# A four-layer image network on one core: layer 1's input and dt products in scan order on two partition halves, and PSUM pairs of layers 2 and 3 read by one engine after the other

## The chip, the core and the metric

The kernel runs on one core of a Trainium2 chip. The metric is the device time of one execution, in microseconds (us), median of the runs. The engines named below are PE (matrix products), DVE (VectorE), ACT (ScalarE), POOL (GpSimd) and SP, whose queue issues nearly all transfers. Each engine takes its instructions strictly in the order in which the program lists them.

## The reference, cut to what matters

The input is 16 images of 96 channels and 56 x 56 positions (L = 3136). Four layers follow each other. Layer 0 is a masked inverted-residual convolution. Layer 1 is a selective scan (below). Layers 2 and 3 each take the Fourier transform of the tokens, a diagonal complex product with ReLU, the inverse transform, and then a small quantized MLP. Everything is float32 but that MLP.

Layer 1, for what the change touches (Din = 192, R = 6, N = 1, four scan directions):

```python
xs = jnp.stack([xf, xt, xf[..., ::-1], xt[..., ::-1]], axis=1)   # xt: the image turned (w before h)
dbl = jnp.einsum('bkdl,kcd->bkcl', xs, x_proj_w)
dts, Bs, Cs = jnp.split(dbl, [R, R + N], axis=2)
dt = jax.nn.softplus(jnp.einsum('bkrl,kdr->bkdl', dts, dt_projs_w) + dt_projs_b[None, :, :, None])
a = jnp.exp(dt[:, :, :, None, :] * A[None, :, :, :, None])
bb = dt[:, :, :, None, :] * Bs[:, :, None, :, :] * xs[:, :, :, None, :]
_, h = jax.lax.associative_scan(comb, (a, bb), axis=-1)
y = jnp.einsum('bkdnl,bknl->bkdl', h, Cs) + Ds.reshape(K, Din)[None, :, :, None] * xs
```

Layers 2 and 3, the part that the change touches (X is the Fourier transform of 192 columns):

```python
xr = jax.nn.relu(X.real * rd - X.imag * idg + rb)
xi = jax.nn.relu(X.imag * rd + X.real * idg + ib)
```

## The kernel before, in words

Three functions run one after the other: `layer0`, `layer1` and `layers23` (layers 2 and 3 together). Inside each, several tasks are written as Python generators. A task yields an `Op` (engine, a cost, a delay, buffers that it takes and gives back), and then issues the instructions of that step. The function `in_order` is a list planner: it always advances the task whose next step can start first by the costs and by the buffers that are free in its books. The order in which the steps come out is the order of the instructions on every engine; there is no other scheduler. So a changed cost, buffer count or step order can move every instruction after it. Which semaphore an instruction waits for is worked out afterwards from the data and the buffers, and not from the costs. Two engines that read the same PSUM tile are also kept apart.

PSUM is used as four pairs of banks (tag `ps`), each of 2 x 512 float32 values per partition.

**Layer 1** has five tasks over the images: `fronts` (norm, in-projection, depthwise convolution, inputs of the scan), `makes` (dt and a), `drives`, `scans` and `backs` (out-projection and MLP).

- The convolution (L783) runs on quarters of the array: 64 rows to 64 columns, four different quarters in turn, into two banks (`p_c`). Its result, u, lies in two tiles: u0 with 128 channels, and u1 with the last 64 channels twice, in its lower half as the image lies and in its upper half turned.
- `inputs` (L811 to L829) makes `proj`, one tile [128, 3136]. Its 128 rows are four groups of 32, one per scan direction, of which 8 are used (6 for dt, then B and C), and one row that `k_one` makes 1 for the dt bias. Seven blocks of 448 columns go through PE, two products each (`xp0`, `xp1`, L819 and L820). ACT writes the lower 64 rows as they come (L822) and the upper 64 rows turned (L827), so that each direction's columns lie in its own order.
- Four transfers (L836) copy the B and C rows to a DRAM tile `bc`; later transfers (`rb`, `rc`, L882 and L886) read them back, spread over 128 partitions.
- `made_of` takes twelve units per image (six channel tiles, two halves of the sequence), each in two pieces of 784 columns. For each piece PE makes two products of 392 columns with all 128 rows of `proj` (L860, `p_d`), ACT takes softplus of the pair (L862, `dt`), and later exp of it (L871, `a`). Softplus, exp and gelu (L1042) need different tables, and a change of table is an instruction of its own.
- DVE multiplies by u (L915), by B (L919), runs the scan (L939, L941), multiplies by C (L946) and adds up (L953, L958). There is one `proj` buffer, five `dt` and two each of `a`, `rb` and `rc`.

**Layers 2 and 3** run three images at a time, as three tasks. `first_half` transposes, multiplies (`p_a` L1262), DVE takes ReLU times the norm (`h`, L1265), PE makes the first transform (`p_1`, L1271), ACT copies it (`y`, L1274) and SP writes it out. `middle` reads it back (`z`) and, in `unit`, makes the second transform in a PSUM pair (L1293) and the complex product: ACT c (L1300), then two child tasks, `imaginary` (DVE L1311 and L1313, ACT L1316, DVE L1318) and `real` (ACT L1322 and L1325, DVE L1327 and L1330), which the planner interleaves freely. Six of these nine read the pair: L1300, L1322 and L1325 on ACT, L1311, L1313 and L1327 on DVE. `back` follows (`p_v` L1341 and L1342, `vv` L1345, `p_u` L1352, `uu` L1355, written out), then `added` reads it back (`z4`) for the last transform (L1388). The tiles `h`, `y`, `vv`, `uu` (two each) and `z4` (three) are of nearly one size and have each their own buffers.

Of the kernel before, what the change touches and what calls it, by code (L numbers as in the profile page):

```python
# [43 lines left out]
ALU = mybir.AluOpType  # L44
# [44 lines left out]
def packed(x):  # L89
# [28 lines left out]
    xp = np.zeros((P, 2 * P), f)  # L118
    wdt = np.zeros((P, 6, P), f)
    o["k_one"] = np.zeros((P, 1), f)  # L120
    for to, k in enumerate((0, 2, 1, 3)):
        xp[32 * to : 32 * to + R + 2, :DIN] = w("x_proj_w")[k]
        o["k_one"][32 * to + R + 2] = 1.0
        for i, halves in enumerate(TILES):
            at = 0
            for of, n in halves:
                if of == k:
                    d = slice(0, P) if n == P else slice(P, DIN)
                    wdt[32 * to : 32 * to + R, i, at : at + n] = w("dt_projs_w")[k, d].T
                    wdt[32 * to + R + 2, i, at : at + n] = w("dt_projs_b")[k, d]  # L130
                at += n
    o["l1_xp0"], o["l1_xp1"], o["l1_dt"] = xp[:, :P].T, xp[:, P:].T, wdt
# [425 lines left out]
def layer1(ctx, tc, src, given, dst):  # L558
# [7 lines left out]
        "ps": 4, "x": 1, "half": 1, "xc": 2, "big": 7, "proj": 1, "dt": 5, "a": 2, "rb": 2, "rc": 2, "xn": 1,  # L566
# [10 lines left out]
    n1, n2, no, xp0, xp1, wdt, kone, ds, fc1b, fc2, fc2b = ph.loads(  # L577
        "l1_n1", "l1_n2", "l1_no", "l1_xp0", "l1_xp1", "l1_dt", "k_one", "l1_d", "l1_fc1b", "l1_fc2", "l1_fc2b"
# [96 lines left out]
    def front(b, it):  # L675
# [135 lines left out]
        it["proj"] = proj = buf([P, L], "proj")  # L811

        def inputs(g):
            banks = 2 if g < 3 else 1
            yield pe(2 * banks, 0.75)
            p = pair("p_x")
            for b in range(banks):
                cols = slice(896 * g + T * b, 896 * g + T * b + T)
                nc.tensor.matmul(p[:, b, :T], xp0, us[0][:, cols], start=True, stop=False)  # L819
                nc.tensor.matmul(p[:, b, :T], xp1, us[1][:, cols], start=False, stop=True)  # L820
            yield act(T * banks, over=0.16)
            nc.scalar.activation(  # L822
                proj[:64, 896 * g : 896 * g + T * banks].rearrange("p (b n) -> p b n", n=T), p[:64, :banks, :T],
                AF.Identity, bias=kone[:64],
            )
            yield act(T * banks, 1.95e-3, give=("ps",))
            nc.scalar.activation(  # L827
                turned(proj[64:])[:, 16 * g : 16 * g + 8 * banks].rearrange("p (b h) w -> p b h w", h=8),
                p[64:, :banks, :T].rearrange("p b (h w) -> p b h w", w=S), AF.Identity, bias=kone[64:],  # L829
            )  # L830

        yield [inputs(g) for g in range(4)]
        it["bc"] = bc = dram.tile([4, 2, L], F32, tag="bc", name="bc")
        yield Op("SP", 1.4, 4.0, post=it["ready"])
        for g in range(4):
            nc.sync.dma_start(bc[g], proj[32 * g + 6 : 32 * g + 8])  # L836
# [6 lines left out]
    def made_of(it):  # L843
# [4 lines left out]
        def steps():  # L848

            for unit in units:  # L850
                i, h = unit
                order = (0, 1) if i < 3 else (1, 0)
                for s in order:
                    yield Op("none", 0.0, 0.0, take=("dt",))
                    made[unit][s] = dt = buf([P, SUB], "dt")
                    yield pe(2, 0.66)
                    p = pair("p_d")
                    for b in range(2):
                        cols = slice(HALF * h + SUB * s + TC * b, HALF * h + SUB * s + TC * b + TC)
                        nc.tensor.matmul(p[:, b, :TC], wdt[:, i], proj[:, cols], start=True, stop=True)  # L860
# [244 lines left out]
def layers23(ctx, tc, src, given, dst):  # L1105
# [9 lines left out]
        "ps": 4, "xn": 2, "xt": 2, "h": 2, "y": 2, "z": 3, "na": 2, "nc": 2, "gg": 6, "vv": 2, "uu": 2,  # L1115
        "z4": 3, "xq": 2, "y16": 2, "h8": 2, "o16": 2, 
    }
    buf = lambda shape, tag, dtype=F32: work.tile(shape, dtype, tag=tag, name=tag, bufs=buffers[tag])

    ident = ph.c([P, P], "ident")  # L1120
# [128 lines left out]
    def first_group(t, w, d1, m0, k, r):  # L1249
# [8 lines left out]
        def quad(at, give):  # L1258
            yield pe(4, 0.325, ("ps", "h"), give)
# [4 lines left out]
            h = buf([Q, 4, HW], "h")  # L1264
# [3 lines left out]
            yield pe(4, 0.325, ("ps",), ("h",))  # L1268
# [3 lines left out]
            yield act(4 * HW, take=("y",), give=("ps",))  # L1272
            y = buf([P, 4, HW], "y")
# [5 lines left out]
            yield Op("none", 0.0, 0.0, give=("y",))  # L1279
# [3 lines left out]
    def middle(w, d1, d2):  # L1283
# [4 lines left out]
        def unit(k, flat, gs, give):  # L1288
# [7 lines left out]
            xr, xi = p[:, :, :S], p[:, :, S:Q]  # L1296
            yield act(448, over=0.25, take=("nc",))
# [3 lines left out]

            open_ = [2]

            def read():
                open_[0] -= 1
                if open_[0] == 0:
                    yield Op("none", 0.0, 0.0, give=("ps",))

            def imaginary():
                yield dve(448, over=0.13)  # L1310
                nc.vector.scalar_tensor_tensor(gi, xi, rd[:, col], c, ALU.mult, ALU.add)  # L1311
                yield dve(448, over=0.13)
                nc.vector.scalar_tensor_tensor(c, xi, rd[:, col], c, ALU.mult, ALU.subtract)  # L1313
                yield from read()
# [5 lines left out]
            def real():  # L1320
                yield act(448, over=0.16)
                nc.scalar.activation(gr, xi, AF.Abs, scale=idg[:, col])  # L1322
                yield act(448, over=0.25, take=("na",))
                a = buf([P, 8, S], "na")
                nc.scalar.activation(a, xr, AF.Relu, bias=rb2[:, col], scale=rd2[:, col])  # L1325
                yield dve(448, over=0.13)
                nc.vector.scalar_tensor_tensor(gr, xr, rd[:, col], gr, ALU.mult, ALU.add)  # L1327
                yield from read()
# [187 lines left out]
```

## Time and profile before

| | us |
|---|---|
| median of 10 runs | 7990.64 |
| lowest and highest | 7981.21, 7999.29 |
| the profiled execution: its time | 7990.78 |
| its span in the profile | 7989.0 |

The same execution by stage (the limits are rounded; busy us of each engine):

| stage, us | PE | DVE | ACT | granted PE clock |
|---|---|---|---|---|
| 0 to 1790, layer 0 | 1686.03 | 1595.39 | 825.81 | 0.98 |
| 1790 to 5290, layer 1 | 3040.23 | 2819.68 | 2475.66 | 0.92 |
| 5290 to 7989, layers 2 and 3 | 2343.35 | 1920.38 | 1637.03 | 0.94 |

A line of the profile's groups reads: line of the kernel, engine, operation, output<-inputs, shape, count | busy us, mean ns of one | idle us of the engine before them and what ended that. A line of waits reads: waiting engine, tile and line <- what it waited for: total us, times, longest. A timeline line begins with the start and the length in us. A float32 product shows as two records of MATMUL, so two products are "x4". In a shape such as 64*64 the first number counts rows of the array, the second columns.

### The profile page before, as it was taken

Reading aid. Unit: us, or ns where it says so; the run is one execution under the profiler, and the core shown is the slowest. Engines: PE = TensorE matmul, PEld = TensorE weight load, DVE = VectorE, ACT = ScalarE, POOL = GpSimd, SP = SyncE. Lnnn points to the kernel's source line nnn. Section 1 sums busy time; section 2 is a strip of 40 time slices with the busy share of each in tenths; the row PEclk is TensorE's granted clock in tenths of the full one; section 3 lists DMA queues with packets and bytes.
Section 4 is the critical chain, followed back from the end, with each engine's and each line's share of the span. In section 5 each row is a group of like instructions: output and inputs, shape, how many; then the busy total and the mean of one; then the engine's idle time right before and its main releaser. Section 6 shows DMA issues by size and latency. Waiting matters only on the chain. (4 is left out here: it accounts for less than half of the span.)

```text
span 7989.0 us, 124748 instructions
## 1 busy us (share of the span) xinstructions
PE 7069.6 (88%) x50410; PEld 4930.4 (62%) x50410; DVE 6335.5 (79%) x8036; ACT 4938.5 (62%) x6249; POOL 999.7 (13%) x798
## 2 busy tenths in 40 slices
PE   7999999987889898888889998768889989998896
PEld 3444444444556566666666665558788878887785
DVE  8999999955888888888888888636777777777765
ACT  4444444436777777777777777425666666666664
POOL 0000000000111111111111111111111111111111
PEclk9999999988899999999999999879899999999997
DMA  1000000013434344434434443235455455555552
GB/s 33 25 24 25 25 25 25 11 30 98 119 113 123 116 122 118 119 117 122 116 116 118 117 116 111 74 80 121 97 121 126 113 119 133 116 118 118 125 116 61
DMA packets 502387, 743.89 MB, mean 93 GB/s; under 512 B 208225, under 2 KB 337553, under 8 KB 498370
## 3 DMA queue, kind: packets, MB, share of 16 engines
q1 hardware_dynamic: 500770, 732.59, 35.4%
q8 instruction: 398, 6.52, 0.3%
q0 software_dynamic: 1040, 3.32, 0.1%
q14 instruction: 179, 1.47, 0.1%
HBM read 543.75 MB, written 191.99 MB: 92 GB/s over the span
## 5 line engine op out<-in xcount | busy, mean ns | idle before, releaser
L509 DVE SCALAR_TENSOR_TENSOR h<-pad,l_dw,h 128x1568 f32<-128x1568 f32 x704 | 1273.2, 1845 | 7.5
L481 PE MATMUL p_c<-pad,taps 64*64 64x392 f32 x8064 | 691.1, 492 | 2.7 <-ACT pad L462 1.9
L1235 POOL TENSOR_TENSOR r<-v,nhalf 112x16 f32<-112x16 f32 (+1 forms) x128 | 398.7, 3119 | 2261.3 <-DVE v L1233 1695.6
L860 PE MATMUL p_d<-proj,l_dt 128*128 128x392 f32 x1536 | 627.9, 536 | 46.1 <-ACT proj L827 13.1
L915 DVE TENSOR_TENSOR dt<-dt,big 128x784 f32<-128x784 f32 x384 | 456.0, 1187 | 219.3 <-ACT a L871 219.2
L481 PEld LDWEIGHTS p_c<-pad,taps 64*64 64x64 f32 x8064 | 300.2, 133 | 383.7 <-issue 354.1
L862 ACT ACTIVATE dt<-p_d 128x784 f32<-128x784 f32 x384 | 314.6, 823 | 240.1 <-PE p_d L860 233.4
L1293 PE MATMUL p<-k_f,z 112*128 112x112 f32 x3072 | 391.4, 289 | 72.7 <-DMA z<-d 57.9
L497 ACT ACTIVATE h<-p_c,shift 128x392 f32<-128x392 f32 x336 | 226.2, 673 | 366.5 <-PE p_c L481 363.0
L860 PEld LDWEIGHTS p_d<-proj,l_dt 128*128 128x128 f32 x1536 | 292.4, 207 | 254.8 <-issue 84.5
L456 PE MATMUL p<-x,l_w 96*128 96x448 f32 (+3 forms) x1280 | 426.5, 513 | 19.1 <-DVE y L546 12.0
L1293 PEld LDWEIGHTS p<-k_f,z 112*128 112x128 f32 x3072 | 384.2, 205 | 80.8 <-issue 50.1
L1048 PE MATMUL p_g<-l_fc,hid 128*112 128x96 f32 x2688 | 380.4, 276 | 43.0 <-ACT hid L1042 34.1
L1341 PE MATMUL p_v<-w,gg 128*112 128x97 f32 x2048 | 374.7, 265 | 26.6 <-DVE gg L1330 14.3
L783 PE MATMUL p_c<-x,taps 64*64 64x392 f32 x4608 | 393.8, 491 | 0.0
L1048 PEld LDWEIGHTS p_g<-l_fc,hid 128*112 128x112 f32 x2688 | 330.4, 188 | 100.9 <-ACT hid L1042 83.5
L804 ACT COPY big<-p_c 64x392 f32<-64x392 f32 (+1 forms) x448 | 267.9, 598 | 175.8 <-PE p_c L783 171.4
L946 DVE TENSOR_TENSOR dt<-a,rc 128x784 f32<-128x784 f32 x384 | 373.3, 972 | 3.8
L1039 PE MATMUL p_f<-zt,w_fc 96*128 96x448 f32 x672 | 329.0, 633 | 51.3 <-ACT zt L1033 51.3
L919 DVE TENSOR_TENSOR dt<-dt,rb 128x784 f32<-128x784 f32 x384 | 372.4, 970 | 2.2
L1342 PE MATMUL p_v<-w2both,gg 128*112 128x97 f32 x2048 | 372.9, 264 | 0.0
L531 PE MATMUL p<-h,l_w 128*96 128x392 f32 x1024 | 363.4, 497 | 10.6 <-ACT h L512 10.6
(283 smaller groups left out, 17173.3 us busy)
## 6 DMA issues: line engine op xcount, KB each, us to landing
rb<-bc SPq DMA_DIRECT2D x256, 392.0 KB
rc<-bc SPq DMA_DIRECT2D x256, 392.0 KB
d<-y SPq DMA_DIRECT2D x448, 192.0 KB
z<-d SPq DMA_DIRECT2D x128, 672.0 KB
rb<-bc SPq DMA_DIRECT2D x256, 196.0 KB
rc<-bc SPq DMA_DIRECT2D x256, 196.0 KB
d<-uu SPq DMA_DIRECT2D x256, 169.8 KB
z<-d SPq DMA_DIRECT2D x192, 194.0 KB
```

The lines of the kernel that those rows point to most:

```text
L456: nc.tensor.matmul(p[n * i : n * i + n, t, :size], w1[:, P * j : P * j + n], images[b]["x"][:, cols], start=True, stop=True,)
L481: nc.tensor.matmul(p[to : to + 64, t, :TC], taps[64 * s : 64 * s + 64, j, i], pad[64 * s : 64 * s + 64, r0 : r0 + 7, i % 3 : i % 3 + S], s ...
L509: nc.vector.scalar_tensor_tensor(out, view, dw[:, j, i : i + 1], out, ALU.mult, ALU.add)
L783: nc.tensor.matmul(p[to : to + 64, b, :TC], taps[64 * s : 64 * s + 64, j, k], pad[64 * s : 64 * s + 64, r0 : r0 + 7, k % 3 : k % 3 + S], s ...
L860: nc.tensor.matmul(p[:, b, :TC], wdt[:, i], proj[:, cols], start=True, stop=True)
L915: nc.vector.tensor_tensor(as_own(dt), as_own(dt), own(u), ALU.mult)
L946: nc.vector.tensor_tensor(dt, a, made["rc", s], ALU.mult)
L1048: nc.tensor.matmul(p[:Q, q, :C], hid[:, j, own], fc2[:, j], start=j == 0, stop=False)
L1235: nc.gpsimd.tensor_tensor(r, v, nhalf[:, :n], ALU.pow)
L1293: nc.tensor.matmul(p[:, q, :Q], flat[:, P * (3 * q + k) : P * (3 * q + k) + P], f2, start=True, stop=True)
L1341: nc.tensor.matmul(out, gs[2 * h][:, at + k], w["w2"][:, 2 * h], start=True, stop=False)
L1342: nc.tensor.matmul(out, gs[1][:, at + k], w["w2both"][:, h], start=False, stop=True)
```

## The change

**Layer 1.** `proj` becomes [128, 1568]: the sequence is cut in eight pieces of 392, even ones on partitions 0 to 63 and odd ones on 64 to 127. Each half holds four directions of 16 rows (8 used, and the bias row). `inputs` becomes two groups; for each of two banks and three weights it makes two products of 392 columns into the two column halves of the array. The second weight reads u0 turned, so the turned directions come out in their own order, and ACT writes each pair with one activation. The B and C rows go out in eight transfers instead of four. A dt piece is two products over 64 rows each (rows 0 to 63 for the first bank, 64 to 127 for the second), with the weights on both halves; the planner's cost of the pair goes from 2 x 0.66 to 1 x 0.7. `proj` gets two buffers.

**Layers 2 and 3.** In `unit`, ACT's three reads of the pair come first, then DVE's three, in one sequence, and only the rest is left to two children. `na` and `nc` get three buffers instead of two. The tiles `h`, `y`, `vv`, `uu` and `z4` are replaced by nine tiles `v` that all five uses take in turn, the one that was given back first being used first.

```diff
 # packed(): weights of layer 1
+    xp = np.zeros((3, P, 64), f)
     for to, k in enumerate((0, 2, 1, 3)):
-        xp[32 * to : 32 * to + R + 2, :DIN] = w("x_proj_w")[k]
-        o["k_one"][32 * to + R + 2] = 1.0
+        own = slice(16 * to, 16 * to + R + 2)
+        xp[to // 2, :, own] = w("x_proj_w")[k, :, :P].T
+        xp[2, 64 * (to // 2) : 64 * (to // 2) + 64, own] = w("x_proj_w")[k, :, P:].T
+        o["k_one"][[16 * to + R + 2, 64 + 16 * to + R + 2]] = 1.0
...
 # layer1
-        "ps": 4, "x": 1, "half": 1, "xc": 2, "big": 7, "proj": 1, "dt": 5, "a": 2, "rb": 2, "rc": 2, "xn": 1,
+        "ps": 4, "x": 1, "half": 1, "xc": 2, "big": 7, "proj": 2, "dt": 5, "a": 2, "rb": 2, "rc": 2, "xn": 1,
...
         def inputs(g):
+            yield pe(6, 0.66)
             p = pair("p_x")
+            for b in range(2):
+                for k in range(3):
+                    for to in range(2):
+                        c = 4 * g + 2 * b + to
+                        u = us[k // 2]
+                        from_ = turned(u)[:, 7 * c : 7 * c + 7] if k == 1 else u[:, TC * c : TC * c + TC]
+                        out = p[64 * to : 64 * to + 64, b, :TC]
+                        if k == 1:
+                            out = out.rearrange("p (w h) -> p w h", h=S)
+                        nc.tensor.matmul(out, xp[:, k], from_, start=k == 0, stop=k == 2)
+            yield act(SUB, over=0.16, give=("ps",))
             nc.scalar.activation(
+                proj[:, SUB * g : SUB * g + SUB].rearrange("p (b n) -> p b n", n=TC), p[:, :, :TC],
+                AF.Identity, bias=kone,
             )
...
         for g in range(4):
-            nc.sync.dma_start(bc[g], proj[32 * g + 6 : 32 * g + 8])
+            for to in range(2):
+                row = 64 * to + 16 * g + 6
+                nc.sync.dma_start(
+                    bc[g].rearrange("k (c n) -> k c n", n=TC)[:, to::2],
+                    proj[row : row + 2].rearrange("k (c n) -> k c n", n=TC),
+                )
...
-                    yield pe(2, 0.66)
+                    yield pe(1, 0.7)
                     p = pair("p_d")
+                    at = (HALF * h + SUB * s) // 2
                     for b in range(2):
-                        cols = slice(HALF * h + SUB * s + TC * b, HALF * h + SUB * s + TC * b + TC)
-                        nc.tensor.matmul(p[:, b, :TC], wdt[:, i], proj[:, cols], start=True, stop=True)
+                        on = slice(64 * b, 64 * b + 64)
+                        nc.tensor.matmul(p[:, b, :TC], wdt[on, i], proj[on, at : at + TC], start=True, stop=True)
...
 # layers23
-        "ps": 4, "xn": 2, "xt": 2, "h": 2, "y": 2, "z": 3, "na": 2, "nc": 2, "gg": 6, "vv": 2, "uu": 2,
-        "z4": 3, "xq": 2, "y16": 2, "h8": 2, "o16": 2, 
+        "ps": 4, "xn": 2, "xt": 2, "v": 9, "z": 3, "na": 3, "nc": 3, "gg": 6, "xq": 2, "y16": 2, "h8": 2, "o16": 2,
...
+    vs = [ph.c([P, 8 * C1], f"v{i}") for i in range(buffers["v"])]
...
-            h = buf([Q, 4, HW], "h")
+            h = quad_of(v)[:Q]
...
 # unit, in its new order
             yield act(448, over=0.25, take=("nc",))
             nc.scalar.activation(c, xr, AF.Identity, bias=ib[:, col], scale=idg[:, col])
+            yield act(448, over=0.16)
+            nc.scalar.activation(gr, xi, AF.Abs, scale=idg[:, col])
+            yield act(448, over=0.25, take=("na",))
+            a = buf([P, 8, S], "na")
+            nc.scalar.activation(a, xr, AF.Relu, bias=rb2[:, col], scale=rd2[:, col])
+            yield dve(448, over=0.13)
+            nc.vector.scalar_tensor_tensor(gi, xi, rd[:, col], c, ALU.mult, ALU.add)
+            yield dve(448, over=0.13)
+            nc.vector.scalar_tensor_tensor(c, xi, rd[:, col], c, ALU.mult, ALU.subtract)
+            yield dve(448, over=0.13, give=("ps",))
+            nc.vector.scalar_tensor_tensor(gr, xr, rd[:, col], gr, ALU.mult, ALU.add)
...
-            v = buf([Q, 8, C1], "vv")
+            v = oct_of(own)[:Q]
...
-            yield Op("SP", 0.7, 5.5, take=("z4",))
-            z = buf([P, 8, C1], "z4")
+            yield Op("SP", 0.7, 5.5, take=("v",))
+            v = vs.pop(0)
+            z = oct_of(v)
```

## The prediction

> **What bounds it now.** I read the page's slices first.
>
> ```profile
> PE   7999999987889898888889998768889989998896
> DVE  8999999955888888888888888636777777777765
> PEclk9999999988899999999999999879899999999997
> ```
>
> No stage has an engine that is simply full: layer 1 (slices 9 to 26) has PE at 8 to 9 and DVE at 8, layers 2 and 3 (the rest) have PE at 9 and DVE at 7. So I cut one repeating stretch out of each. In layer 1 five successive stretches of 208.2 us hold the same counts, one image each; in layers 2 and 3 two images repeat every 317.5 us. From the windows view (span, then PE, PEld, DVE, ACT, POOL busy, clock, DMA):
>
> ```profile
> 3429.20:3637.40 208.20, 188.19 (x1300) 126.65 (x1299) 176.61 (x212) 155.49 (x192) 33.74 (x31) 0.94 0.40 117
> 6125.40:6442.90 317.50, 286.40 (x2334) 256.58 (x2333) 238.22 (x386) 204.02 (x276) 49.97 (x16) 0.98 0.53 121
> ```
>
> In both PE is busiest, at 90%, and loses the rest to waits. DVE follows at 85% in layer 1. What DVE and ACT wait for in layer 1 (the first line over four images, the second over one; total, times, longest):
>
> ```profile
> DVE dt L915 <- ACT a L871: 68.0, 32, 8.2
> ACT dt L862 <- PE p_d L860: 16.9, 10, 4.0
> ```
>
> DVE stands 17.0 us per image for the exp of dt, out of 31.6 idle; ACT stands 16.9 us for the dt product that PE has not come to. PE is the late one. The groups of one image that the change touches, in the same view (count, then busy us and mean ns):
>
> ```profile
> L860 PE MATMUL p_d<-proj,l_dt 128*128 128x392 f32 x98 | 40.5, 538 | 2.2 <-DVE v L999 1.0 <-ACT half L759 0.9 <-ACT dt L862 0.4
> L862 ACT ACT_TABLE_LOAD x13 | 16.7, 1283 | 0.2
> L827 ACT ACTIVATE proj<-p_x,k_one 64x896 f32<-64x896 f32 (+1 forms) x4 | 6.7, 1720 | 0.1
> L822 ACT ACTIVATE proj<-p_x,k_one 64x896 f32<-64x896 f32 (+1 forms) x4 | 3.5, 906 | 0.1
> ```
>
> **Layer 1, dt products.** A pair of products is four records. From the timeline (start, length):
>
> ```profile
> 3009.30 1.48 PE L860 MATMUL p_d<-proj,l_dt 128*128 128x392 f32 x4
> 3010.62 0.74 PE L1048 MATMUL p_g<-l_fc,hid 128*112 128x96 f32 x6
> ...
> 4824.18 6.16 PE L783 MATMUL p_c<-half,taps 64*64 64x392 f32 x72
> 4830.27 1.58 PE L860 MATMUL p_d<-proj,l_dt 128*128 128x392 f32 x4
> 4831.78 6.16 PE L783 MATMUL p_c<-x,taps 64*64 64x392 f32 x72
> 4837.76 6.11 PE L783 MATMUL p_c<-half,taps 64*64 64x392 f32 x72
> 4843.80 1.58 PE L860 MATMUL p_d<-proj,l_dt 128*128 128x392 f32 x4
> ```
>
> A pair costs 1.32 us start to next start. Do two 64-row halves run side by side? The convolution answers: 72 records of the same 392 columns on quarters of the array take 5.98 us (4831.78 to 4837.76), not 72 x 0.33 = 23.8, so four quarters overlap, among them both row halves into the same columns and different banks, as the new pair does. I take 0.66 us per pair: 24 pairs x 0.66 = 15.8 us less PE per image.
>
> Changing the way the array is split costs something: p_d to p_c takes 1.51 us instead of 1.32, and p_c to p_d 6.09 (4824.18 to 4830.27) where p_c to p_c takes 5.98: 0.19 and 0.11, on average 0.15. By the order of the changed program there are 319 runs of dt products; 261 lie between full-array products (two new changes each), 30 have one such side, so 552 new changes. At 0.15 that is 83 us over 16 images, 5.2 per image. Net 10.6 us per image; bounds 9.2 (all at 0.19) and 15.8 (none).
>
> The Trainium skill, "TensorEngine Tiling (Array Packing)", Key Properties, says that changing the tiling mode drains TensorE. That speaks against this change; the rows above show the price at 0.11 to 0.19 us. The page has no figure for it.
>
> **Layer 1, inputs.** Out go 14 products of 448 columns, 0.75 us each by the timeline (10.5). In come 24 of 392 columns, two column halves side by side: 12 x 0.66 = 7.9, and 0.6 for four changes. Eight of them (four slots) read u turned, each element 224 bytes on, which no PE row shows. The nearest rows are ACT's: 1.72 turned (L827) against 0.91 plain (L822), 1.9 times. So 0 to 0.6 x 4 = 2.4; I take 2.4, since DVE's turned rows pay too. Net 10.9 - 10.5 = 0.4 more PE work. ACT loses 6.7 + 3.5 = 10.2 us and gets 2 activations of 784 columns, 0.82 each by L862's activation: 8.6 less. The order has 34 more table loads, 34 x 1.283 = 43.6 us, 2.7 per image: ACT goes from 155.5 to about 149.6 and stays under the others. SP issues 8 bc transfers instead of 4, about 0.25 us each, ahead of the rb and rc reads queued behind them: 1 us once per image, hidden since the second proj tile lets them go out before the old image's last exp; without that cover it is 1 us per image, 16 in all.
>
> The Trainium skill, "ScalarE: Activation LUTs", What ACT_TABLE_LOAD costs, adds a drain of about 1.38 us to each load. Here an exp starts 0.01 us after its load (3028.11 + 1.28, then 3029.40) and the load 0.02 us after the activation before it, so no drain shows; by the page the 34 loads would be 90 us, also on an engine with room.
>
> **Layer 1, sum.** PE falls from 188.2 to 188.2 - 10.6 + 0.4 = 178.0 us, level with DVE's 176.6. Two ways to price that. Directly: eight stops of DVE per image, each served 0.36 (0.66 less two changes) to 0.66 us earlier: 2.9 to 5.3. By load: now the busiest engine fills 188.2/208.2 = 0.904 of the period; at the same share 178.0 gives 196.9, 11.3 us less. The cap is the whole 17.0. I take 9, near the load figure, because PE's queue gets ahead and not only the one product shorter. dt products run from 1847 to 5073 in the trace, 15.5 periods: 15.5 x 9 = 140. The first image's inputs lie bare (p_x starts at 1831.3, bc goes out at 1845.9): about 5 us less. What is late next: DVE itself.
>
> **Layers 2 and 3.** Now both engines take turns on one PSUM pair; waits of two periods:
>
> ```profile
> ACT gg L1322 <- DVE gg L1311: 16.0, 24, 1.1
> ACT na L1325 <- DVE gg L1311: 8.1, 12, 0.8
> DVE nc L1313 <- ACT na L1325: 19.3, 26, 1.3
> ACT y L1274 <- DMA d<-y: 6.2, 5, 2.1
> ...
> PE p_v L1341 <- DVE gg L1330: 3.7, 2, 1.8
> PE p_v L1341 <- DVE gg L1327: 1.6, 4, 0.4
> PE p_x L1457 <- DVE gg L1327: 1.1, 2, 0.5
> ```
>
> L1322 needs nothing of L1311, nor L1313 of L1325, except the pair. Three reads by ACT and then three by DVE leave one handover. The first three lines are 43.4/2 = 21.7 us per period, but on engines with 79 (DVE) and 113 us (ACT) to spare. What reaches PE are the last three: 6.4/2 = 3.2 us per period. From 5303 to 7946 there are 8.3 periods: 27 us. Moving DVE's first read behind two more ACT reads (637 and 730 ns in the groups view) delays gi, which PE only needs at p_v; the third na and nc tiles cover that, and without them it is up to 1.4 us per unit on ACT and DVE, not on PE.
>
> The shared v tiles: by the order, 125 of 224 products h (DVE) now also wait for a transfer, and 51 of 128 evacuations v (ACT); none did. Behind h on DVE stands every other image's work, and p on PE waits for h. Nine tiles in turn should be long released; I take 0. The nearest row is y's own wait: 6.2/5 = 1.24 us each.
>
> **Sum.** The profiled execution took 7990.78 us, 0.14 over the median, span 7989.0. 7990.8 - 140 - 5 - 27 = 7819.
>
> **Rivals.** (B) DVE packs tightly: PE ahead everywhere, all 17.0 us gone, 15.5 x 17.0 = 264, and a third of PE's 31.1 idle in layers 2 and 3, 10 x 8.3 = 83: 7990.8 - 264 - 5 - 83 = 7639. For it: nothing else makes DVE wait over 4 us per image. Against: layer 1 never fills an engine past 0.904.
>
> (C) Only the direct term comes. The clock could do it: at 2100 to 2300 us PE is busy 0.86 and the clock is 0.90, against 0.94 at 0.904, so a PE with more gaps is a slower PE; 4% of 178.0 is 7 us, most of the 10.2 gained. Then 15.5 x 2.9 = 45, 5 and nothing in layers 2 and 3: 7941.
>
> (D) Slower: h on DVE waits for transfers of the tile's last user. 28 x 125/224 = 15.6 such waits per period; at 2.1 us, y's longest, and with no slack left before PE, 32.8 x 8.3 = 272 against 145: 8118. At 1.24 us it is 161, 8007. It decides from about 1.1 us per wait. Against: PE stands for h only 3.5 us in two periods.
>
> (E) The halves do not run side by side. Then PE gets 5.2 (changes) and 8.3 (24 x 0.66 + 0.6 + 2.4 - 10.5) more: 201.7/0.904 = 223.1, 14.9 x 15.5 = 231 later: 8195 with the 27. The quarters of the convolution speak against it.
>
> **Chances.** Forecast 0.55 (7819, its own range 7740 to 7900), B 0.14, C 0.17, D 0.10, E 0.04. The range 7635 to 8005 takes in C and B, and leaves out E and most of D. A run of this kernel tells 0.2%, 16 us, from no change. Faster: forecast, B and nearly all of C, 0.83; within 0.2%: 0.04, the edges of C and D; slower 0.13.
>
> **What would show it.** Right: p_d on 64 rows with 0.66 to 0.85 us start to next; PE near 178 and the layer-1 period near 199; DVE's wait for exp near 8 us per image; no waits between ACT's and DVE's first reads of a pair. Wrong: p_d still 1.3; the clock well below 0.94 in layer 1; DVE h or ACT v ended by DMA for more than 10 us per period; the period of layers 2 and 3 above 317.5.

## The result, and the profile after

The changed kernel takes 8161.93 us in the median of 8 runs (8127.41 to 8177.35), the kernel before 7989.69: a ratio of 1.0209, with an interval of 1.0198 to 1.0219. It is slower by 172 us, where 171 us less had been forecast. One of the four executions of a later kernel (order and shared tiles, 7921.04) ran at a granted clock of 0.818 instead of 0.942 and took 8523.04 us; its ratio leaves it out, and without it the median is 7919.22.

The profiled execution took 8177.35 us, with a span of 8175.6, 186.6 us over that of before. Cut at the first product `p_a` of layers 2 and 3, this divides as follows: layers 0 and 1 end at 5528.0 instead of 5314.3 (214 later), and layers 2 and 3 take 2647.6 instead of 2674.7 (27 less). So the forecast for layers 2 and 3 came out to the microsecond, by luck, as the experiments show, and the loss lies in layer 1.

The slices of the page after:

```profile
PE   7999999987888888888888888658899998999996
DVE  8999999937877777777877777945777777677765
PEclk9999999987899888888888888768999999999997
```

In layer 1 (slices 9 to 27 here) DVE fell from 8 to 7, and the clock from 9 to 8: everything there is less dense, PE as well as DVE. The windows view of 2500 to 5000 us, which is layer 1 in both kernels (span, then PE, PEld, DVE, ACT, POOL busy, clock, DMA), after:

```profile
2500.00:5000.00 2500.00, 2156.05 (x14662) 1382.44 (x14664) 1934.36 (x2323) 1673.13 (x2096) 473.74 (x331) 0.86 0.37 107
```

and before:

```profile
2500.00:5000.00 2500.00, 2247.20 (x15425) 1507.94 (x15424) 2131.00 (x2535) 1870.30 (x2304) 407.48 (x350) 0.94 0.40 117
```

DVE issues 2323 instructions instead of 2535 in the same time, 8% fewer, and PE, DVE and ACT all wait more. What the waits end on, in the same window (total, times, longest), after:

```profile
DVE dt L924 <- ACT a L880: 259.4, 65, 15.9
DVE z L1060 <- PE p_g L1058: 111.3, 41, 8.8
DVE v L1007 <- ACT o L999: 92.4, 48, 5.1
...
ACT o L999 <- PE p_o L994: 161.4, 41, 8.5
ACT dt L871 <- PE p_d L869: 62.3, 65, 2.7
ACT L871 <- DVE big L967: 48.5, 10, 5.2
ACT L880 <- DVE a L950: 43.3, 22, 3.5
...
PE p_o L994 <- ACT ysq L984: 84.2, 22, 5.1
```

and the same pairs before (DVE, ACT, PE; L915 is now L924, L862 is L871, L871 is L880):

```profile
DVE dt L915 <- ACT a L871: 185.8, 87, 11.3
DVE z L1051 <- PE p_g L1049: 46.6, 30, 5.8
DVE v L998 <- ACT o L990: 36.0, 24, 5.0
...
ACT dt L862 <- PE p_d L860: 195.8, 113, 5.1
ACT o L990 <- PE p_o L985: 56.8, 34, 3.8
...
PE p_o L985 <- ACT ysq L975: 25.6, 20, 1.8
```

The wait that the change aims at has shrunk as meant: ACT stands 62.3 us for `p_d` instead of 195.8. But DVE's wait for exp of dt has grown, with fewer and longer stops (259.4 us in 2500/226.3 = 11 periods, 23.5 us each, where about 8 had been forecast; before, 185.8 in 12 periods, 15.5 each), and a circle of waits through the out-projection and the MLP has grown with it: DVE for `p_g` and `o`, ACT for `p_o`, PE for `ysq`. The two lines "ACT L871" and "ACT L880" have no tile: they are table loads. The groups view of the whole execution shows how ACT stands before them, after (last column: idle time before, and what ended it):

```profile
L871 ACT ACT_TABLE_LOAD x244 | 313.1, 1283 | 55.9 <-DVE big L967 51.5 <-DVE big L962 0.4
L880 ACT ACT_TABLE_LOAD x192 | 246.3, 1283 | 100.1 <-DVE a L950 67.5 <-DVE dt L955 23.1 <-DVE a L948 7.1
```

and before:

```profile
L862 ACT ACT_TABLE_LOAD x216 | 277.1, 1283 | 4.1
L871 ACT ACT_TABLE_LOAD x192 | 246.3, 1283 | 41.5 <-DVE a L941 26.2 <-DVE dt L946 7.2 <-DVE a L939 4.9
```

The idle time of ACT before these loads goes from 45.6 to 156.0 us. ACT reaches the softplus and exp of coming units while DVE still works on the tiles that they would overwrite, and everything that stands behind them in ACT's queue, `ysq`, `o` and gelu among it, waits too.

### The profile page after: what moved, and what is told of

Same layout as the page of the kernel before. It is cut to its first block, busy times and chain, and to the rows that moved or that the text cites. A ratio compares the mean times of both kernels' runs of the same rounds, so it can differ in the third digit from the quotient of the medians.

```text
span 8175.6 us, 125724 instructions
## 1 busy us (share of the span) xinstructions
PE 7128.4 (87%) x50730; PEld 4910.9 (60%) x50730; DVE 6309.4 (77%) x8036; ACT 4833.3 (59%) x6187; POOL 1081.5 (13%) x798
## 5 line engine op out<-in xcount | busy, mean ns | idle before, releaser
L924 DVE TENSOR_TENSOR dt<-dt,big 128x784 f32<-128x784 f32 x384 | 455.1, 1185 | 360.2 <-ACT a L880 359.7
L1246 POOL TENSOR_TENSOR r<-v,nhalf 112x16 f32<-112x16 f32 (+1 forms) x128 | 373.2, 2925 | 2257.4 <-DVE v L1244 1583.2
L1057 PE MATMUL p_g<-l_fc,hid 128*112 128x96 f32 x2688 | 432.0, 301 | 50.3 <-ACT hid L1051 44.8
L1048 PE MATMUL p_f<-zt,w_fc 96*128 96x448 f32 x672 | 390.0, 732 | 78.2 <-ACT zt L1042 78.2
L1057 PEld LDWEIGHTS p_g<-l_fc,hid 128*112 128x112 f32 x2688 | 376.7, 212 | 114.8 <-ACT hid L1051 100.6
L994 PE MATMUL p_o<-ones,ysq 128*112 128x96 f32 x1792 | 298.2, 295 | 110.9 <-ACT ysq L984 105.8
L869 PE MATMUL p_d<-proj,l_dt 64*128 64x392 f32 x1536 | 382.5, 593 | 12.7 <-DVE v L1008 5.9
L871 ACT ACTIVATE dt<-p_d 128x784 f32<-128x784 f32 x384 | 312.1, 822 | 124.7 <-PE p_d L869 96.0
L1277 DVE SCALAR_TENSOR_TENSOR v<-p_a,r 112x768 f32<-112x768 f32 x224 | 212.2, 954 | 214.5 <-PE p_a L1274 213.7
L1274 PE MATMUL p_a<-first,xt 97*112 97x192 f32 x1792 | 358.1, 356 | 21.1 <-ACT z L1472 10.9
```

The source lines that it names most:

```text
L869: nc.tensor.matmul(p[:, b, :TC], wdt[on, i], proj[on, at : at + TC], start=True, stop=True)
L924: nc.vector.tensor_tensor(as_own(dt), as_own(dt), own(u), ALU.mult)
L1048: nc.tensor.matmul(ps[j // 2][:, j % 2, :T], w_fc1[:, P * j : P * j + P], zt, start=True, stop=True)
L1057: nc.tensor.matmul(p[:Q, q, :C], hid[:, j, own], fc2[:, j], start=j == 0, stop=False)
L1246: nc.gpsimd.tensor_tensor(r, v, nhalf[:, :n], ALU.pow)
```

## The experiments

Layer 1 is given in the tables by its steady figures per image, worked out from the trace records between the fourth and the third-last image (by the choice of the instruction that marks an image they move by up to some 1 us): the period, PE's busy time, and the time that PE's clock was granted at half rate ("half clock"; the records of the clock hold only full and half rate).

### Which part of the program loses

**Layers 2 and 3 alone.** Layer 1 is that of before, all of `layers23` is that of after. As an edit of the changed kernel:

```diff
-layer1, packed weights of layer 1: after
+layer1, packed weights of layer 1: before
```

> Layer 1 as before the change, layers 2 and 3 as after it. The profile of the changed kernel puts layers 2 and 3 at 2647.6 us against 2674.7, and layer 1 at 214 us more. If the two halves of the change don't touch each other: 7990 - 27 = 7963 us. If the gain of layers 2 and 3 only exists behind the new layer 1 (another start of the images), it stays at 7990.

7965.09 us, ratio 0.9967 (0.9956 to 0.9978): 25 us less than before. Hence the changed layer 1 costs 8162 - 7965 = 197 us.

**A lower planned cost and nothing else.** On top of that kernel, only the planner's number for the old dt pair; every instruction is the same as before, and only the order differs.

```diff
-                    yield pe(2, 0.66)
+                    yield pe(1, 0.7)
```

> As r1_layers23_only, with one number changed: the planner counts a pair of dt products in layer 1 at 0.7 us instead of 1.32, while PE still does them in full. Theory 'order' (the planner's list, made with costs that the chip doesn't keep, puts steps into the queues too early and they block what stands behind): this alone makes layer 1 slower, by 100 to 200 us, about 8060 to 8160. Theory 'clock' (PE has more gaps since it has less to do, is throttled, and every chain through it gets longer): PE's work is the same, so it stays near 7963.

8142.52 us (1.0174 to 1.0206), 177 more than without it; the period goes from 208.2 to 225.3. One planner's cost that no instruction carries out moves nearly as much time as the whole change.

**One `proj` tile** in the changed kernel:

```diff
-"proj": 2
+"proj": 1
```

> The changed kernel with one proj tile instead of two. Theory 'proj' (two tiles let the inputs of the next image come early, between the steps of the running one): most of the 214 us of layer 1 come back, 7970 to 8020. Theories 'order' and 'clock': stays within 60 us of 8162.

8027.62 us (1.0031 to 1.0063): 134 less than the changed kernel.

**True costs for the planner.** If the list is bad because its costs are too low, the measured ones should mend it.

```diff
-            yield pe(6, 0.66)
+            yield pe(6, 0.95)
...
-                    yield pe(1, 0.7)
+                    yield pe(1, 0.86)
```

> The changed kernel with the planner's costs as the profile of the changed kernel measured them: 0.86 us for a pair of dt products (was 0.7) and 5.7 us for a group of inputs (was 3.96). No instruction changes but its place. Theory 'order': half or more of the 214 us come back, 8060 or less. Theory 'clock': the work and the gaps stay, so it stays within 60 us of 8162.

8184.88 us (1.0226 to 1.0262): no better. So it is not these two wrong costs that make the list bad.

**Buffer and cost, crossed.** Two more kernels plan the new pair at the old 1.32 us, with one and with two `proj` tiles.

```diff
-                    yield pe(1, 0.7)
+                    yield pe(2, 0.66)
```

> The changed kernel with one proj tile and a dt pair counted at 1.32 us; inputs counted as in the change. Of the four corners two are known: two tiles and 0.7 is 8162, one tile and 0.7 is 8028. If the two parts add up and the cost matters as in r2 (177 us): 7965 to 7990. If every other list is as good or as bad by chance: anywhere between 7980 and 8160.

> The changed kernel with two proj tiles and a dt pair counted at 1.32 us. If the second tile is what hurts: 8100 to 8180, as with 0.7. If the low cost is what hurts: 8030 or less.

| median, us | pair planned at 0.7 | at 1.32 |
|---|---|---|
| two `proj` tiles | 8161.93 | 8113.81 |
| one `proj` tile | 8027.62 | 8016.98 |

The second tile costs 134 us (97 at the higher cost), the lower cost 48 us (11 with one tile). They act on the list in different ways, as the order of ACT's records shows. With one tile, the next image's inputs come only behind all 24 dt pieces of the running image; with two, at either cost, behind one of them, and then only 5 dt pieces of the next image stand before the running image's first out-projection, where before there were 17. The low cost alone (the run above) puts all 24 there.

### What the new work is worth in the old order

**New work, old order.** The inputs are issued as four groups of one bank, planned like the old ones, with one `proj` tile and the pair at 2 x 0.66. Then all else of layer 1 comes out in the order of before.

```diff
-            yield pe(6, 0.66)
+            banks = 2 if g < 3 else 1
+            yield pe(2 * banks, 0.75)
...
-        yield [inputs(g) for g in range(2)]
+        yield [inputs(g) for g in range(4)]
...
-                    yield pe(1, 0.7)
+                    yield pe(2, 0.66)
```

> The changed kernel with the planner of layer 1 led through the same steps as before the change: one proj tile, a dt pair counted at 1.32 us, four groups of inputs counted as before (each now makes one bank, so ACT writes four times 392 columns). All other instructions of layer 1 stand in the order of before; the work is the new one: dt products side by side, turned reads, no turned writes. Theory 'order': the new work alone is no loss, so 7965 us or less; if the term of the prediction for it (9 us per image) was right in this order, 7965 - 140 = 7825. Theory 'clock' (less work makes gaps, gaps throttle PE): above 7990 even in the old order, with the clock of layer 1 well under 0.92.

The same with the dt products over all 128 rows, so that the pair costs as much as before (it leaves out the split into row halves, so dt is another sum):

```diff
-  matmul(p[:, b, :TC], wdt[on, i], proj[on, at : at + TC], ...)
+  matmul(p[:, b, :TC], wdt[:, i], proj[:, at : at + TC], ...)
```

> r5_new_work_old_order (7976) with the dt products over all 128 rows, one after the other, as in r6. It leaves out the split of the halves, so dt is the sum of two pieces. Only the side-by-side products differ from r5, in the same order. If they are worth the 10.6 us of PE per image that the prediction counted: 7976 + 100 or more. If PE's time in layer 1 is given back as half-clock time: equal to r5 or up to 30 us faster, with the half-clock time near 24 us per image instead of 40.

| | median, us | ratio, interval | period | PE per image | half clock |
|---|---|---|---|---|---|
| before's layer 1 | 7965.09 | 0.9956 to 0.9978 | 208.2 | 187.4 | 24.2 |
| new inputs, full-array dt | 7966.11 | 0.9963 to 0.9983 | 208.2 | 187.6 | 23.2 |
| new inputs, dt on row halves | 7976.45 | 0.9972 to 0.9995 | 208.2 | 183.9 | 39.6 |

(The first row is the first experiment, with PE's figure from the kernel before.) The last two are the plainest answer to the forecast. In one and the same order, the row halves take dt work from PE, 3.7 us per image by its busy time, since some of the saving is lost to the clock (below), and the period does not move: 208.21 us in all three. The waits of the last one in 2500 to 5000 us, to be held against those of before:

```profile
DVE dt L922 <- ACT a L878: 157.6, 58, 9.6
...
ACT dt L869 <- PE p_d L867: 148.7, 81, 4.3
```

DVE waits 28 us less for exp in twelve periods, and ACT 47 us less for `p_d`; elsewhere in the circle other waits grow (DVE for `p_g` from 46.6 to 69.1, ACT for `p_o` from 56.8 to 94.4). And the changed kernel is 185 us slower than this one with the same products: that is the price of its list, with the planner's entries and the grouping of the inputs that make it.

### The clock

**Full-array dt in the new order**, the same edit in the changed kernel (again without the split):

> The changed kernel in its own order, but each dt product takes all 128 rows again, one after the other, in the full-array shape: 1.32 us per pair instead of 0.86, no change of the array's split. It leaves out the split of the halves, so dt is the sum of two pieces. If side by side is worth something in this order: 24 pairs x 0.46 = 11 us per image on PE, up to 170 us more, 8330. Theory 'order': PE isn't what is late, so within 60 us of 8162. Theory 'clock': more PE work keeps the clock up, so equal or faster than 8162.

**Every dt pair issued twice** in the changed kernel:

```diff
-                    for b in range(2):
+                    for b in (0, 1, 0, 1):
```

> The changed kernel with every side-by-side dt pair issued twice into the same banks (24 x 0.66 = 16 us more PE work per image, the same order and the same number of changes of the array's split). If the changes of split are what makes side by side slower than full-array in this order (r6, 8126): 8162 or up to 100 us more. If PE's idle time and the clock are: about 8126, with the half-clock time falling from 65 to about 31 us per image as in r6.

**Idle products** in the back groups, where PE waits: four per group, 28 per image, about 21 us, in the changed order and in the old one.

```diff
+            for j in range(2):
+                nc.tensor.matmul(p[:C1, :4, :Q], w_out[:, 0], y0[:, cols], start=True, stop=True)
...
+            nc.tensor.matmul(p[:, 0, :T], w_fc1[:, :P], x[:C], start=True, stop=True)
...
+            nc.tensor.matmul(ps[0][:, 0, :T], w_fc1[:, :P], x[:C], start=True, stop=True)
```

> The changed kernel in its own order with extra products that nobody reads, four of 448 columns (0.75 us each) per group of the out-projection and MLP step, put where PE waits for ACT or DVE (before the out-projection, the transposes and the first MLP product); each is overwritten by the real product. 28 x 0.75 = 21 us more PE work per image. Theory 'clock': the gaps are filled, the half-clock time of 65 us per image falls to 40 or less, and the time falls by 50 us or more, to 8110 or less. Theory 'order' alone: no gain, 8162 to 8350.

> r5_new_work_old_order with the same extra products. Theory 'clock': faster than r5 by 20 us or more. Theory 'order' alone: PE gets 21 us more per image and is near 188 again, so equal to r5 or up to 100 us slower.

| | median, us | against | period | PE per image | half clock |
|---|---|---|---|---|---|
| changed kernel | 8161.93 | | 226.3 | 194.9 | 64.8 |
| full-array dt | 8126.15 | -36 | 219.6 | 193.1 | 31.0 |
| pairs twice | 8145.46 | -17 | 223.0 | 197.9 | 29.2 |
| idle products | 8205.97 | +44 | 226.5 | 204.1 | 32.6 |
| old order, new work | 7976.45 | | 208.2 | 183.9 | 39.6 |
| the same, idle products | 8043.57 | +67 | 212.8 | 199.2 | 24.9 |

With more dt work on PE the changed kernel is not slower, and with the full array it is faster by 36 us (ratio 1.0149 to 1.0181 against 1.0198 to 1.0219). Issued twice, it is 17 us less by the medians, but the intervals overlap (1.0181 to 1.0212), so a gain isn't shown there. The windows of 2500 to 5000 us of these two, to hold against 0.86 after:

```profile
2500.00:5000.00 2500.00, 2194.33 (x14923) 1437.96 (x14915) 1986.21 (x2389) 1718.31 (x2148) 484.31 (x338) 0.93 0.39 110
```

```profile
2500.00:5000.00 2500.00, 2219.14 (x15918) 1413.39 (x15916) 1955.38 (x2349) 1702.50 (x2126) 475.13 (x333) 0.94 0.38 109
```

The clock is back at 0.93 and 0.94, and DVE gets more done (2389 and 2349 instead of 2323). So more work on PE does bring its clock back. How much of the loss the clock is isn't settled: the 36 us of the full array may also come from the changes of split that it does without, and the run with every pair twice, which keeps them, lies at 8145 between the values that the two causes called for (8126, and 8162 or more). It is no remedy in general: the idle products bring the clock back as well, and the kernels get 44 and 67 us slower, probably since these products stand in the chain of waits. Nor does the clock explain most of the loss, for the runs with a clock of 0.93 or 0.94 are still 136 us or more above before.

### What sets the old order's period

To see whether PE sets it at all, softplus was replaced by exp, so that no change of table lies between the two (it leaves out softplus). The base is the 7935.87 us kernel of the next part.

```diff
-                        ..., p[:, :, :TC], AF.Softplus
+                        ..., p[:, :, :TC], AF.Exp
```

> r12_unit_order_only (7936) with exp in the place of softplus in layer 1, so that ACT needs no change of table between dt and a. It leaves out the softplus (dt is another function). The order of all instructions stays; about 18 of 33 table loads per image go, 18 x 1.28 = 23 us of ACT. If the chain PE to ACT to DVE (DVE's 17 us of waiting for exp) sets the period: 8 to 17 us per image less, 7670 to 7810. If DVE's own work or PE sets it: within 40 us of 7936.

7844.76 us (ratio 0.9808 to 0.9858), 91 less than its base. Table loads fall from 33.0 to 15.7 per image, 17.3 x 1.283 = 22 us of ACT, and the period falls to between 198 and 201 us. ACT had been busy 156 of 208 us. Work taken from it shortens the period, by some 8 us for 22: the low edge of the 8 to 17 us per image that the chain called for, with a total between its 7810 and the 7896 that the rival reached down to. The 3.7 us taken from PE, at 187 of 208, did not. PE is not out of the circle, though: the idle products, 15 us more of PE in the old order, lengthened the period by 4.6.

### Layers 2 and 3, part by part

Three parts of the change meet here: the read order, the shared tiles, and the third `na` and `nc`. All of these runs have before's layer 1.

The read order alone, with own tiles and two `na` and `nc` (the planner's cost of the last DVE step, L1330, falls by 0.06 us with it); then the nine shared tiles alone, with the free order of reads. As edits of the kernel before:

```diff
 # read order alone: ACT's three reads, then DVE's three, in unit's own sequence
+            yield act(448, over=0.16)
+            nc.scalar.activation(gr, xi, AF.Abs, scale=idg[:, col])
...
+            yield dve(448, over=0.13, give=("ps",))
+            nc.vector.scalar_tensor_tensor(gr, xr, rd[:, col], gr, ALU.mult, ALU.add)
...
 # shared tiles alone
-"h": 2, "y": 2, ... "vv": 2, "uu": 2, "z4": 3
+"v": 9
```

> The kernel before with one change: in layers 2 and 3 ACT's three reads of a PSUM pair come first and then DVE's three; all tiles as before (two na, two nc). The prediction gave the whole 27 us of layers 2 and 3 to this: 7963. If the shared tiles (or the third na and nc) are what helped: 7985 to 8010.

> The kernel before with one change: in layers 2 and 3 the nine shared tiles in the place of h, y, vv, uu and z4 (two na, two nc, reads of the pair free as before). r12 has the read order at 7936, r1 has both (and the third na and nc) at 7965. If the parts add up: 7990 + 29 = 8019, with DVE and ACT waits for transfers. If the tiles cost nothing as the prediction said: 7990.

Order and shared tiles, but two `na` and `nc`; shared tiles and three `na` and `nc`, but the free order:

```diff
-"na": 3, "nc": 3
+"na": 2, "nc": 2
```

> Before's layer 1; layers 2 and 3 with the new read order and the nine shared tiles, but na and nc with two buffers as before. Measured so far, against 7990: the read order alone 7936 (54 less), the shared tiles alone 8075 (85 more), all three together 7965 (25 less). Theory 1, the third na and nc carry the difference: the two parts add, 7990 - 54 + 85 = about 8020. Theory 2, the read order repairs what the shared tiles break and the third na and nc do little: within 15 us of 7965. A value between 7980 and 8005 would leave both with a share.

> Before's layer 1 and before's free order of reads in layers 2 and 3, with the nine shared tiles and three buffers of na and nc. Theory 1, the third na and nc repair the shared tiles by themselves: about 8075 - 56 = 8019 or less. Theory 2, it is the read order that repairs them: within 15 us of 8075.

| median, us | free order of reads | ACT's reads, then DVE's |
|---|---|---|
| own tiles, two `na` and `nc` | 7990 (before) | 7935.87 (0.9919 to 0.9944) |
| shared tiles, two | 8075.02 (1.0093 to 1.0126) | 7921.04 (0.9899 to 0.9939) |
| shared tiles, three | 8189.54 (1.0240 to 1.0271) | 7965.09 (0.9956 to 0.9978) |

The read order is worth 54 us with own tiles, 154 with the shared ones and 224 with the third `na` and `nc`. The shared tiles cost 85 us in the free order and nothing in the new one (15 us less by the medians, but the intervals overlap). The third `na` and `nc` cost 115 and 44 us. So neither theory of the last pair held: the order does repair the shared tiles, but the third buffers harm in both. 7921 us is the fastest kernel of the study that leaves nothing out, some 65 us under before.

The waits of DVE in 5600 to 7600 us with order, shared tiles and three buffers:

```profile
DVE t L1395 <- PE p L1391: 150.5, 35, 11.6
DVE v L1268 <- PE p_a L1265: 148.0, 83, 7.3
```

and with two:

```profile
DVE t L1395 <- PE p L1391: 18.2, 26, 0.9
DVE v L1268 <- PE p_a L1265: 11.7, 13, 4.4
```

Not every wait shrinks with two. The first of these has grown, from 167.9, and the second is new:

```profile
DVE gg L1314 <- ACT na L1312: 199.4, 25, 15.0
DVE y L1434 <- ACT y L1432: 55.2, 49, 3.2
```

A likely reading is that with three buffers the units' steps run ahead in the list, and the other two images' steps on DVE then stand for products that come late; the lists of these two kernels were not compared.

### All planner's books back at once

The changed kernel with everything that it issues, but with one `proj` tile, two `na` and `nc`, and the pair planned at 1.32 us:

```diff
-"proj": 2    ... "na": 3, "nc": 3
+"proj": 1    ... "na": 2, "nc": 2
...
-                    yield pe(1, 0.7)
+                    yield pe(2, 0.66)
```

> The changed kernel with everything that it issues, but with the planner's books of before: one proj tile, two na and nc tiles, and the dt pair planned at 1.32 us. Theory: the loss lies in the two added buffers and the lower cost, and stages add because they follow each other: 8017 (one proj tile and cost 1.32 with three na and nc tiles) less 44 (7965 to 7921, the third na and nc tiles) is 7973, 189 less than the changed kernel and 0.2% under the kernel before. Rival: what is left of the change's own step structure in layer 1 weighs more in this list, or the stages share something at their border: over 8000.

7972.66 us in 11 runs, ratio 0.9978 (0.9969 to 0.9987): 189 us under the changed kernel and 17 under before. The sum of the single experiments was 7973. So these three entries cost 189 us, more than the whole loss of 172. That a cost can do it through the order alone is shown by the run in which nothing else changed (177 us); for the buffers, order and reuse of the tiles were not told apart. But these entries are not all that layer 1 lost. With before's layer 1 and the same layers 2 and 3 the time is 7921, so the new layer 1 still costs some 50 us here, and the kernel comes out level with before only by the gain behind it. Of layer 1's 197 us, 145 are the second tile and the low cost (8162 to 8017), 41 the new input steps' own list (8017 to 7976) and 11 the new work in the old order (7976 to 7965).

## Why the prediction was wrong, point by point

- **The pair on row halves: right.** From the timeline after (start, length), a pair takes 15.55 - 14.69 = 0.86 us to the next start, changes of split included; of the 188 pairs that run at full clock with a product right behind them, 186 take this time. 1.32 - 0.86 = 0.46, times 24, is 11.0 us per image; the steps gave 10.6. Rival E is out.

```profile
3014.69 0.93 PE L869 MATMUL p_d<-proj,l_dt 64*128 64x392 f32 x4
3015.55 0.59 PE L1039 MATMUL p_t<-ident,zn 112*96 112x112 f32 x4
```

- **The inputs' turned reads: about right.** In the records, a turned read takes 0.71 us from start to next start, a plain one 0.33 to 0.35: some 3.0 us more per image, where 2.4 was taken. The issue of the eight `bc` transfers was mis-sized more: at some 0.64 us each it takes 5.2 us per image, where four had taken 1.9 to 3.4 and 1 us more was forecast.
- **PE at 178.0: right in work, wrong in time.** In the old order PE was busy 183.9 us, with 39.6 - 24.2 = 15.4 us more at half clock. PE was busy for some 12 us of these (about 34 us of the half clock against 22), and half of them is time that the clock added: 183.9 - 6 is about 178. In the changed kernel PE was busy 194.9 us with 64.8 at half clock. Rival C had this mechanism nearly at its size: it let the clock take back 7 us of the 10.2 gained, and in the old order it took about 6. But C kept the direct term of 45 us, which did not come, and had no loss from the list.
- **"At the same share 178.0 gives 196.9": the step that failed first.** It took the busiest engine for the one that sets the period. In the same order, with less PE work, the period stayed at 208.21 us, so the term of 140 us was worth nothing; even the 3.7 us that PE's busy time fell should have given 3.7/0.904 = 4.1 per period by that rule. DVE's stand for exp was read as PE being late; the run without softplus tables shows that the circle goes through ACT, whose queue holds softplus, exp and gelu in a fixed order. DVE's work was not taken away in any run. The direct price, 2.9 to 5.3 us per period, was too high as well.
- **The new list taken as harmless: the step that decided the sign.** The prediction took the changed program's order to count split changes and table loads, and never asked what it does to the waits. It gave the second `proj` tile credit, for hiding 1 us; that tile costs 97 to 134 us. The planned cost of the pair, 11 to 48 us, was not priced at all. What is left of the new input steps' own list is about 41 us (8017 against 7976 in the old order). No rival had a slower kernel by this way.
- **34 table loads hidden on ACT: true of their time, not of their place.** ACT's busy time per image fell to 150.8 us, near the 149.6 forecast. The loads themselves are 1.283 us each, with no drain to be seen. But ACT now stands before them for DVE's tiles, 156.0 us in place of 45.6 at the softplus and exp loads.
- **Layers 2 and 3, -27: right in sum by luck, from wrong terms.** The handovers went, as forecast. Before, in 5600 to 7600 us, there were these waits, and the first two have no like after:

```profile
ACT gg L1322 <- DVE gg L1311: 47.7, 73, 1.1
DVE nc L1313 <- ACT na L1325: 57.9, 78, 1.3
DVE gg L1311 <- ACT nc L1300: 82.0, 26, 8.7
```

  In the place of the third, DVE's first read now waits for ACT's last one (same stretch, after):

```profile
DVE gg L1323 <- ACT na L1321: 141.3, 22, 12.9
```

  That is longer, on an engine with room. The read order was worth 54 us by itself, twice the 27 that were read off the three lines reaching PE, so those lines were not the whole of it; the order of all that follows changed too. The third `na` and `nc`, entered as the cover of this step, cost 44 us, and these two misses happen to leave about the sum that was forecast. The shared tiles at 0 were right in the new order only.
- **Rival D, `h` standing for transfers: wrong.** With the shared tiles alone, in the old free order, it is 12.5 us in 5600 to 7600 us, against 32.8 per period in the rival's sum:

```profile
DVE v L1268 <- DMA d<-v: 12.5, 4, 3.1
```

This wait is too short for the 85 us of that kernel; what makes them was not taken apart further. In the changed kernel it is 0.4 us.

**What stays open.** Which list is better is shown by the waits named and by experiments, not by a rule: the two true costs gave no better list, and nothing here ranks lists beforehand. That half clock follows from PE's gaps is shown by the runs that fill them; how much of the 172 us the clock costs, and how the gaps and the circle of waits feed each other in the changed order, was not taken apart further. Nor is it known whether the old period held at 208.21 us because PE doesn't set it, or also because of the whole windows of the last part.

## What to carry to other kernels

Where a planner or a list fixes the order on every engine, a buffer count or a cost is an edit of the whole program: price the new work in the old order first, then the new order with the old work, and distrust a buffer that only lets one task run ahead. A busy share says which engine is fullest, not which one sets the period; take work from one engine at a time and see what moves. Test the parts of a change apart and together: here one part gained 54 to 224 us depending on the others, and a buffer that looked like cover cost 44.

## What the runs showed of the hardware

- **The clock can undo a saving.** PE's clock records show full and half rate only, in windows of 3.413 us; of the full-rate windows of before between the first image's out-projection and that of the second-last image, none of the 663 in which PE was busy 0.7 or more was followed by half rate, all 34 below 0.4 were, and 27 of the 61 between. Once at half rate, even windows busy over 0.9 were at times followed by another (15 of 75). Less dt work in the same order raised the half-clock time from 23.2 to 39.6 us per image. The Trainium skill, "TensorE: Matmul & The Clock Gate", HAM oscillation, tells of kernels whose PE falls back to half rate while it waits; these runs agree, and add that a saving on PE alone can bring more of it.
- **Where a period is steady, it is a whole number of these windows:** 208.21 us (before, and seven runs with its order of layer 1) is 61.0 of them, 218.5 (two `proj` tiles, pair planned at 1.32) is 64.0, 225.3 (the low cost alone) is 66.0; without softplus tables two images take 399.4, which is 117.0, and in layers 2 and 3 two images take 317.5 before, which is 93.0, and 307.2 with the read order alone, which is 90.0. The changed kernel does not settle (226.3 is 66.3). This may be why 208.21 us didn't move under small savings; the cause was not tried by itself.
- **Reading a moving operand 224 bytes apart** takes PE 0.71 us per record of 392 columns instead of 0.33 to 0.35, by the records of the changed kernel's inputs.
